# Sampling of the first image taken in turn with the offsets of the other three

## The chip, the cores and the metric

The kernel runs on one core of one Trainium2 chip. The metric is the device time of one execution in microseconds (us), lower is better. Before the change, three runs took 10536.02 to 10541.7 us, with a median of 10539.41 us. A core has five engines that run beside each other, each with its own queue of instructions in a fixed order: PE (matmul), DVE (vector), ACT (scalar functions), POOL (general) and SP (here it only starts transfers). Sixteen DMA engines move data between HBM and the core's SBUF.

## The reference

The input x holds four images of 64x64 positions with 256 channels. Layer 0 is a deformable convolution, layer 1 an attention and a feed-forward block with a choice of tokens. Only layer 0 is touched here. Cut to what matters:

```
def layer0(x):                                   # per image
    v = group_norm(x)                            # 32 groups of 8 channels
    xp = v @ in_w + in_b                         # projection that is sampled
    x1 = silu(batch_norm(depthwise_conv3x3(v)))
    offset = x1 @ off_w + off_b                  # 8 groups x 9 points x (x, y)
    mask = softmax(x1 @ mask_w + mask_b)         # over the 9 points
    out = sum over points of mask * bilinear(pad(xp), point + offset)
    return x + (out @ out_w + out_b)
```

An offset smaller than one position in size reaches only a 5x5 window around a position. The kernel therefore makes, for each position and group, 25 window weights out of mask and offset, and a sample is a weighted sum of 25 shifted copies of xp. The few positions with a larger offset are computed once more, exactly, by gathers.

## The kernel before, in words

The program is written as dataflow, and a scheduler decides at build time in which order each engine gets its instructions. It takes ready instructions by their place in the program, by a model of durations. What is wrapped in `keep` stays in the program's order on its engine. `Pinned` is a stand-in for `nc.vector` that wraps every DVE operation in `keep`.

**Offsets** (`offsets_and_weights`, L263) runs first, for all four images, with `slab` 8: an image is 32 tiles of 128 positions, worked on in four slabs of 8. Its parts:

- `front(n)` (L322): loads x in eight pieces (`xt`, L333, on SP's queue, three buffers), transposes them on PE, takes statistics on DVE (L341) and copies to `xn` on ACT; then group statistics, and the scaling of the whole of `xn` on ACT (L366). The front of the next image is advanced by one or two pieces after each slab.
- `convolution(s)` (L412): channel half 1 on PE by nine matmuls with diagonal matrices `diag` (L420), channel half 0 on DVE by nine multiply-adds (L432, L434), then silu on ACT.
- `taps(s)` (L437): offset and mask matmuls into `po` (L444), the sum `raw` on DVE (L448), the softmax's maximum and subtraction on DVE, its exponential on ACT (L458).
- `window(s)` (L461): the rest of the softmax (L463 to L465), the hat functions on ACT (L473 to L477), three rounds of `my`, `mxy` and sums into `w5` on DVE (L483 to L488), transposes on PE (L497) and the store of the weights `wt_d` (L501).
- `projection(i)` (L380): matmuls of a quarter of an image (L387), bias on ACT into `xp`, stores of `xp_d` (L398), transposes (L405), copies into `tb` on ACT (L406), and the store of the gather table `tab_d` (L407).

All stores are issued on SP. Per slab the program has convolution(s+1), taps(s), window(s), projections and the next front. [...] four for `a_t` (transposes), four for `a_m` (matmul results). `a_ld` (xt, tb, wT) has three buffers.

**Zero fill** (L1387 to L1397) follows: 24 stores on SP put zeros on the borders of `xp_d` and `tab_d`.

**Sampling of image 0** (`sample_image`, L668) runs alone after that, with depth 6. It is a generator with some 440 steps. `list_tokens` makes the list of positions with large offsets. Then for each of four chunks of 1024 positions and each channel half: the shifted source `xs` is loaded (L683, two buffers), and for each of 25 window places the weights `wb` are loaded with a broadcast (L688, twelve buffers) and multiplied with the source (L697, kept) and added to `ac` (L705, kept). Between them `exact_rows` gathers table rows with POOL's indirect DMAs (L626) and reduces them on DVE (L637, L640). At a chunk's end `ac` is multiplied with the output weights (L721), x and bias are added (L725, L728) and `t_d` is stored (L729).

**Attention and the rest** start with `t_d` of image 0. The sampling of image n+1 is taken in turn with attention of image n; there `sample_image` has depth 1, so `wb` has two buffers and `xs` and `ac` one.

The main program's part:

```
    with scope(
        ("a_one", 1, 0), ("a_xn", 2, 0), ("a_ld", 3, 0), ("a_wk", 2, 0), ("a_w1p", 1, 0), ("a_sm", 2, 0),
        ("a_t", 4, 1), ("a_m", 4, 1),
    ):
        offsets_and_weights(range(NB), SLAB, 2)
    ...
    with scope(("smp", 2, 0), ("two", 2, 0), ("sb", 2, 0), ("dn", 1, 0), ("ps_m", 2, 1)):
        for _ in sample_image(0, 6):
            pass
```

Of the kernel before, what the change touches and what calls it, by code (L numbers as in the profile page):

```python
# [16 lines left out]
P = 128  # L17
# [28 lines left out]
def layers_kernel(ctx: ExitStack, tc: tile.TileContext, a, out: bass.AP):  # L46
# [216 lines left out]
    def offsets_and_weights(images, slab, rows_bufs):  # L263

        ca = S.a_one
# [52 lines left out]
        diag = ca.tile([P, K2, P], F32, name="diag")  # L318
        for tap in range(K2):
            nc.vector.tensor_scalar(diag[:, tap], ident, dwk[:, 1, tap : tap + 1], None, ALU.mult)  # L320

        def front(n):  # L322
# [8 lines left out]
            for s in range(8):  # L331
                xt = S.a_ld.tile([P, 4, C], F32, tag="xt", name="xt")
                nc.sync.dma_start(  # L333
                    out=xt, in_=x_d[n, s * 512 : (s + 1) * 512].rearrange("(t p) c -> p t c", p=P)
                )
                for k in range(CC):
                    pt = S.a_t.tile([P, 4, P], F32, tag="pt", name="pt")
                    for t in range(4):
                        nc.tensor.transpose(pt[:, t, :], xt[:, t, k * P : (k + 1) * P], ident)
                    ptf = pt.rearrange("p t q -> p (t q)")  # L340
                    nc.vector.bn_stats(st[:, k, s, :], ptf)  # L341
                    nc.scalar.copy(
                        xn[:, k, 1 + 8 * s : 9 + 8 * s, 1 : 1 + W],
                        ptf.rearrange("p (r w) -> p r w", w=W),
                    )
                yield
            mv = S.a_sm.tile([P, CC, 2], F32, tag="mv", name="mv")
            for k in range(CC):
                nc.vector.bn_aggr(mv[:, k, :], st[:, k].rearrange("p s f -> p (s f)"))
# [5 lines left out]
            nc.vector.tensor_copy(gm, pg)  # L355
            gv = S.a_sm.tile([P, CC], F32, tag="gv", name="gv")
            nc.vector.tensor_sub(gv, mv[:, :, 0], gm)
            nc.vector.tensor_mul(gv, gv, gv)
            nc.vector.tensor_add(gv, gv, mv[:, :, 1])
# [3 lines left out]
            nc.vector.scalar_tensor_tensor(gm, gm, -1.0, gr, ALU.mult, ALU.mult)  # L363
# [7 lines left out]
        for _ in front(images[0]):  # L371
            pass
        for at, n in enumerate(images):
            xn = xns.pop(n)
            after = front(images[at + 1]) if at + 1 < len(images) else iter(())
# [4 lines left out]
            def projection(s):  # L380
# [16 lines left out]
                for f in range(CC):  # L397
                    nc.sync.dma_start(out=xp_d[n][f][:, q0 : q0 + 16 * MP], in_=xp[:, f, : 16 * MP])  # L398
                for o in range(0, 16 * MP, P):
# [7 lines left out]
                    nc.sync.dma_start(out=tabw[q0 + o : q0 + o + m], in_=tb[:m].rearrange("p f g c e -> p (f g c e)"))  # L407
# [4 lines left out]
            def convolution(s):  # L412
                x1 = S.a_wk.tile([P, CC, slab * P], F32, tag="x1", name="x1")
                x1s[s] = x1
                r0 = 2 * slab * s
                for o in range(0, slab * P, 512):
                    pc = S.a_m.tile([P, 8, W], F32, tag="pm", name="pc")
                    for tap in range(K2):
                        r = r0 + o // W + tap // 3
                        nc.tensor.matmul(  # L420
                            pc, diag[:, tap], xn[:, 1, r : r + 8, tap % 3 : tap % 3 + W],
                            start=(tap == 0), stop=(tap == K2 - 1),
                        )
                    nc.scalar.activation(
                        x1[:, 1, o : o + 512], pc.rearrange("p r w -> p (r w)"), AF.Silu,
                        bias=bnsh[:, 1:2], scale=bns[:, 1:2],
                    )
                acc = x1[:, 0].rearrange("p (r w) -> p r w", w=W)
                for tap in range(K2):
                    src = xn[:, 0, r0 + tap // 3 : r0 + tap // 3 + 2 * slab, tap % 3 : tap % 3 + W]  # L430
                    if tap == 0:
                        nc.vector.tensor_scalar(acc, src, dwk[:, 0, 0:1], None, ALU.mult)  # L432
                    else:
                        nc.vector.scalar_tensor_tensor(acc, src, dwk[:, 0, tap : tap + 1], acc, ALU.mult, ALU.add)  # L434
                nc.scalar.activation(x1[:, 0], x1[:, 0], AF.Silu, bias=bnsh[:, 0:1], scale=bns[:, 0:1])

            def taps(s):  # L437
                x1 = x1s.pop(s)
                raw = S.a_wk.tile([P, slab, 3 * GP], F32, tag="raw", name="raw")
                for t in range(0, slab, 2):  # L440
# [7 lines left out]
                    nc.vector.tensor_tensor(  # L448
# [7 lines left out]
                nc.vector.tensor_reduce(red, m3, AX.X, ALU.max)  # L456
                nc.vector.tensor_tensor(m3, m3, rbc, ALU.subtract)
# [3 lines left out]
            def window(s):  # L461
                raw, m3, red, rbc = raws.pop(s)
                nc.vector.tensor_reduce(red, m3, AX.X, ALU.add)  # L463
                nc.vector.reciprocal(red, red)
                nc.vector.tensor_tensor(m3, m3, rbc, ALU.mult)  # L465
# [10 lines left out]
                nc.vector.tensor_reduce(omax[:, n, s * slab : (s + 1) * slab], hat[:, 1], AX.X, ALU.max)  # L476
# [4 lines left out]
                for ey in range(3):  # L481
                    my = S.a_w1p.tile([P, slab, GP], F32, tag="my", name="my", bufs=2)
                    nc.vector.tensor_mul(my, raw[:, :, 2 * GP :], hat[:, ey, :, GP:])  # L483
                    for ex in range(3):
                        mxy = S.a_w1p.tile([P, slab, GP], F32, tag="mxy", name="mxy", bufs=2)
                        nc.vector.tensor_mul(mxy, my, hat[:, ex, :, :GP])
                        blk = w5[:, :, ex : ex + 3, ey : ey + 3]
                        nc.vector.tensor_tensor(  # L488
                            blk, blk, mxy.rearrange("p t (g i j) -> p (t g) i j", i=3, j=3), ALU.add
                        )  # L490

                w5t = w5.rearrange("p (t f g) i j -> p t f (g i j)", t=slab, f=CC)
                for t in range(0, slab, 4):
                    for f in range(CC):
# [6 lines left out]
                        nc.sync.dma_start(out=wt_d[n][f, :, o : o + 512], in_=wT[: GH * ND])  # L501
# [3 lines left out]
            for s in range(ns):  # L505
                if s + 1 < ns:
                    convolution(s + 1)
                taps(s)
                window(s)
                for i in range(s * (H // 16) // ns, (s + 1) * (H // 16) // ns):  # L510
                    projection(i)
                for _ in range(8 // ns):
                    next(after, None)
            for _ in after:
                pass

# [151 lines left out]
    def sample_image(n, depth=1):  # L668
# [9 lines left out]
        for c in range(L // CH):  # L678
            ac = S.dn.tile([P, CC, CH], F32, tag="ac", name="ac", bufs=min(depth, 2))
            for f in range(CC):  # L680
                xs = S.dn.tile([P, CH // W + 4, MP], F32, tag="xs2", name="xs2", bufs=min(depth, 2))
# [4 lines left out]
                for d in range(ND):  # L686
                    wb = S.dn.tile([P, CH], F32, tag="wb", name="wb", bufs=2 * depth)
# [6 lines left out]
                    else:  # L694
                        prt = S.dn.tile([P, CH], F32, tag="prd", name="prd", bufs=min(depth, 2))
# [685 lines left out]
    with scope(  # L1381
        ("a_one", 1, 0), ("a_xn", 2, 0), ("a_ld", 3, 0), ("a_wk", 2, 0), ("a_w1p", 1, 0), ("a_sm", 2, 0),
        ("a_t", 4, 1), ("a_m", 4, 1),
    ):
        offsets_and_weights(range(NB), SLAB, 2)

    with scope(("one", 1, 0)):  # L1387
        zm = S.one.tile([P, 2 * G * 2 * CG], F32, name="zm")
        nc.gpsimd.memset(zm, 0.0)
        for n in range(NB):  # L1390
            tabw = tab_d[n].rearrange("(q g) c -> q (g c)", g=G)
            for q0 in (0, (H + 2) * MP):
                for f in range(CC):
                    nc.sync.dma_start(out=xp_d[n][f][:, q0 : q0 + 2 * MP], in_=zm[:, : 2 * MP])
                nc.sync.dma_start(
# [3 lines left out]
    with scope(("smp", 2, 0), ("two", 2, 0), ("sb", 2, 0), ("dn", 1, 0), ("ps_m", 2, 1)):  # L1399
        for _ in sample_image(0, 6):  # L1400
# [77 lines left out]
```

## Time and profile before

| | us |
|---|---|
| Median of three runs | 10539.41 |
| The profiled execution | 10563.61 |
| Its span, first to last instruction | 10561.9 |
| Constants and first front, until the first convolution | 0 to 59 |
| Offsets of four images | 59 to 814 |
| Zero fill and list of positions | 814 to 872 |
| Sampling of image 0 | 872 to 1482 |
| Attention's preparation of image 0, then all the rest | from 1482 |

The profile records one execution. Over the whole span the engines are busy like this (busy us, share of the span, instructions):

```profile
PE 9008.4 (85%) x38460; PEld 4375.8 (41%) x38460; DVE 8547.2 (81%) x13406; ACT 7377.6 (70%) x8389; POOL 5265.2 (50%) x3059
```

Most of that is attention, so these shares say little of the first 1482 us. There one reads by stage. In a group's line, what stands after the second bar is how long the engine stood idle just before these instructions, and after the arrow who ended that idle time. PE's clock is granted[...]: 1.00 is full speed.

### The profile page before, as it was taken

To read this page: it belongs to the slowest core of one execution; us is meant where nothing else is said; L and a number is where in the kernel's file an instruction comes from. 1 tells how busy PE (TensorE), PEld (TensorE's weight loads), DVE (VectorE), ACT (ScalarE), POOL (GpSimd) and SP (SyncE) were. 2 spreads that over 40 slices of the span, in tenths; PEclk is the share of its full clock that TensorE was granted. 3 is DMA by queue.
4 is the path that set the end of the run, shared out by engine and by line. 5 is a ranking of instruction groups with operands and counts; after the bars stand their busy time and mean duration, and the time that the engine had idled before them with its cause. 6 is when DMAs were issued, how large, how long until landed. Compare 5 with 4: busy or idle time off the path is not lost. (4 is left out here: it accounts for less than half of the span.)

```text
span 10561.9 us, 115936 instructions
## 1 busy us (share of the span) xinstructions
PE 9008.4 (85%) x38460; PEld 4375.8 (41%) x38460; DVE 8547.2 (81%) x13406; ACT 7377.6 (70%) x8389; POOL 5265.2 (50%) x3059
## 2 busy tenths in 40 slices
PE   7882029999999678999999589999999699999995
PEld 4551014444444343444444344444444344444443
DVE  7776879898989778989899679899898357777772
ACT  4450018888888528888888438888888379999991
POOL 0004307676555326767655327676555155555552
PEclk8985569999999889999999789999999799999997
DMA  3336752222222252212111352222111300000002
GB/s 119 107 138 180 206 167 70 61 67 64 70 64 73 98 167 60 52 55 58 51 55 50 116 152 53 53 54 54 52 59 41 101 13 9 10 8 7 7 5 75
DMA packets 381330, 766.00 MB, mean 73 GB/s; under 512 B 49105, under 2 KB 212593, under 8 KB 380689
## 3 DMA queue, kind: packets, MB, share of 16 engines
q1 hardware_dynamic: 324432, 678.78, 20.3%
q0 software_dynamic: 30144, 45.87, 2.9%
q10 hardware_dynamic: 26112, 33.56, 0.9%
q8 instruction: 309, 5.06, 0.2%
q14 instruction: 333, 2.72, 0.1%
HBM read 580.88 MB, written 177.14 MB: 72 GB/s over the span
## 5 line engine op out<-in xcount | busy, mean ns | idle before, releaser
L909 DVE TENSOR_TENSOR r<-nn,r 128x512 f32<-128x512 f32 x6144 | 3943.0, 683 | 861.5 <-PE nn L904 805.9
L904 PE MATMUL nn<-qn,kf 32*128 32x512 f32 (+1 forms) x12288 | 4518.8, 640 | 132.7 <-DVE r L909 95.8
L994 POOL TENSOR_TENSOR r<-r 128x1024 f32<-128x1024 f32 x1024 | 2708.8, 2645 | 2645.4 <-DVE r L909 2625.3
L988 ACT ACTIVATE r<-d 128x1024 f32<-128x1024 f32 x3072 | 3117.2, 1015 | 1085.4 <-DVE r L998 699.9
L894 PE MATMUL d<-qf,kf 32*128 32x512 f32 (+1 forms) x12288 | 3338.1, 632 | 76.5 <-DMA qf<-qf 43.1
L990 ACT ACTIVATE r<-r 128x1024 f32<-128x1024 f32 x3072 | 3124.1, 1051 | 32.6
L904 PEld LDWEIGHTS nn<-qn,kf 32*128 32x128 f32 (+1 forms) x12288 | 1399.4, 185 | 1902.1 <-DVE r L909 1450.5
L932 PE MATMUL pv<-v,et 128*128 128x257 f32 x8192 | 2105.3, 400 | 15.0 <-DVE acv L956 15.0
L932 PEld LDWEIGHTS pv<-v,et 128*128 128x128 f32 x8192 | 1507.6, 194 | 975.5 <-issue 768.6
L894 PEld LDWEIGHTS d<-qf,kf 32*128 32x128 f32 (+1 forms) x12288 | 1018.0, 186 | 1340.3 <-issue 736.1
L996 POOL TENSOR_TENSOR r<-r 128x512 f32<-128x512 f32 x1024 | 1335.8, 1304 | 92.7 <-DVE r L909 17.1
L705 DVE TENSOR_TENSOR ac<-ac,prd 128x1024 f32<-128x1024 f32 x768 | 991.8, 1291 | 8.8
L697 DVE TENSOR_TENSOR prd<-xs,wb 128x1024 f32<-128x1024 f32 x768 | 977.7, 1273 | 15.2 <-DMA wb<-wt 12.0
L626 POOL DMA_INDIRECT ga<-tab,tii x576 | 718.3, 1247 | 207.3 <-issue 117.7
L916 ACT ACTIVATE et<-et,nshift 128x512 f32<-128x512 f32 x1024 | 723.8, 707 | 28.2 <-DVE et L1001 28.2
L998 DVE TENSOR_TENSOR r<-r 128x512 f32<-128x512 f32 x1024 | 723.6, 707 | 4.1 <-POOL r L994 3.7
L1001 DVE TENSOR_TENSOR et<-r 128x512 f32<-128x512 f32 x1024 | 698.1, 682 | 0.4
L115 ACT ACT_TABLE_LOAD x9 | 11.5, 1283 | 799.3 <-DVE mv L259 703.0
L721 PE MATMUL pmo<-outwp,ac 128*128 128x256 f32 x512 | 135.7, 416 | 469.1 <-DVE ac L705 431.2
L480 POOL MEMSET w<- 128x1600 f32 x16 | 22.9, 1432 | 675.0 <-PE ptw L497 352.3
L721 PEld LDWEIGHTS pmo<-outwp,ac 128*128 128x128 f32 x512 | 100.8, 205 | 521.4 <-DVE ac L705 304.5
L420 PE MATMUL pc<-xn,diag 128*128 128x512 f32 x576 | 262.2, 609 | 33.4 <-ACT xn L366 33.4
(344 smaller groups left out, 5282.7 us busy)
## 6 DMA issues: line engine op xcount, KB each, us to landing
wb<-wt SPq DMA_DIRECT2D x800, 512.0 KB
tab<-tb SPq DMA_DIRECT2D x128, 256.0 KB
v<-t SPq DMA_DIRECT2D x64, 512.0 KB
xs<-xp SPq DMA_DIRECT2D x32, 680.0 KB
xp<-xp SPq DMA_DIRECT2D x32, 544.0 KB
xt<-in_x_dram SPq DMA_DIRECT2D x32, 512.0 KB
xr<-in_x_dram SPq DMA_DIRECT2D x64, 256.0 KB
t<-xr SPq DMA_DIRECT2D x64, 256.0 KB
```

Of the source, the lines that this page charges most:

```text
L697: keep(nc.vector.tensor_tensor(pr.rearrange("p (r w) -> p r w", w=W), src, wb.rearrange("p (r w) -> p r w", w=W), ALU.mult,))
L705: keep(nc.vector.tensor_add(ac[:, f, :], ac[:, f, :], pr))
L894: keep(nc.tensor.matmul(d[:, j, :], kf[g, blk, rows(kt)], qs[q][0][g, blk, :], start=True, stop=True))
L904: keep(nc.tensor.matmul(nn, kf[g, blk, rows(kt)], qs[q][1][g, blk, :], start=True, stop=True))
L909: keep(nc.vector.tensor_tensor(r[:, j, :], ns[j], r[:, j, :], ALU.mult))
L916: keep(nc.scalar.activation(ets[b], ets[b], AF.Exp, bias=nshift))
L932: keep(nc.tensor.matmul(pv, ets[b0 + i][:, rows(j)], v[:, k0 + i, :], start=(i == 0), stop=(i == PVB - 1)))
L988: keep(nc.scalar.activation(rs[b, p], ds.pop((b, p)), AF.Ln))
L990: keep(nc.scalar.activation(rs[b, p], rs[b, p], AF.Exp, scale=-1.0))
L994: keep(nc.gpsimd.tensor_tensor(rs[b, 1], rs[b, 1], rs[b, 2], ALU.add))
L996: keep(nc.gpsimd.tensor_tensor(rs[b, 1][:, 0], rs[b, 1][:, 0], rs[b, 3][:, 0], ALU.add))
L998: keep(nc.vector.tensor_add(rs[b, 1][:, 1], rs[b, 1][:, 1], rs[b, 3][:, 1]))
```

## The change

The sampling of image 0 no longer waits for the offsets of all images. `offsets_and_weights` becomes a generator. It runs image 0 to its end (`next(others)`), and then the offsets of images 1 to 3 and the sampling of image 0 are advanced in turn: after each of five places in a slab, three or four steps of sampling.

With that go these edits:

- slabs of four tiles in place of eight;
- for images 1 to 3 both channel halves of the convolution run on PE (`diag` holds both); image 0 keeps half 0 on DVE;
- taps(s) stands ahead of convolution(s+1);
- for images 1 to 3 the DVE operations are pinned to the written order (`vec`);
- x is loaded on POOL's queue; the stores of projection, table, window weights and the zero fill are issued on ACT's queue; sampling's loads and stores and the store of `raw` stay on SP;
- fewer buffers: `wb` 2 for 12, `xs` and `prd` 1 for 2, `a_ld` 2 for 3, `my` and `mxy` 1 for 2, `xp` 1 for 2; PSUM 3 + 3 + 2 banks, where offsets had 4 + 4;
- the zero fill stands before the offsets.

```diff
-        diag = ca.tile([P, K2, P], F32, name="diag")
-        for tap in range(K2):
-            nc.vector.tensor_scalar(diag[:, tap], ident, dwk[:, 1, tap : tap + 1], None, ALU.mult)
-
-        def front(n):
+        diag = ca.tile([P, CC, K2, P], F32, name="diag")
+        for k in (1, 0):
+            for tap in range(K2):
+                nc.vector.tensor_scalar(diag[:, k, tap], ident, dwk[:, k, tap : tap + 1], None, ALU.mult)
+
+        def front(n, vec):
...
-                nc.sync.dma_start(
+                nc.gpsimd.dma_start(
                     out=xt, in_=x_d[n, s * 512 : (s + 1) * 512].rearrange("(t p) c -> p t c", p=P)
                 )
...
-        for _ in front(images[0]):
+        for _ in front(images[0], nc.vector):
             pass
         for at, n in enumerate(images):
             xn = xns.pop(n)
-            after = front(images[at + 1]) if at + 1 < len(images) else iter(())
+            vec = pinned if at else nc.vector
+            after = front(images[at + 1], vec) if at + 1 < len(images) else iter(())
...
-                    nc.sync.dma_start(out=xp_d[n][f][:, q0 : q0 + 16 * MP], in_=xp[:, f, : 16 * MP])
+                    nc.scalar.dma_start(out=xp_d[n][f][:, q0 : q0 + 16 * MP], in_=xp[:, f, : 16 * MP])
...
-                    nc.sync.dma_start(out=tabw[q0 + o : q0 + o + m], in_=tb[:m].rearrange("p f g c e -> p (f g c e)"))
+                    nc.scalar.dma_start(out=tabw[q0 + o : q0 + o + m], in_=tb[:m].rearrange("p f g c e -> p (f g c e)"))
...
+                for k in range(CC):
+                    if k == 0 and not at:
...
+                                vec.scalar_tensor_tensor(
+                                    acc, src, dwk[:, 0, tap : tap + 1], acc, ALU.mult, ALU.add
+                                )
+                        nc.scalar.activation(x1[:, 0], x1[:, 0], AF.Silu, bias=bnsh[:, 0:1], scale=bns[:, 0:1])
+                        continue
+                    for o in range(0, slab * P, 512):
+                        pc = S.a_m.tile([P, 8, W], F32, tag="pm", name="pc")
+                        for tap in range(K2):
+                            r = r0 + o // W + tap // 3
+                            nc.tensor.matmul(
+                                pc, diag[:, k, tap], xn[:, k, r : r + 8, tap % 3 : tap % 3 + W],
+                                start=(tap == 0), stop=(tap == K2 - 1),
+                            )
...
                         blk = w5[:, :, ex : ex + 3, ey : ey + 3]
-                        nc.vector.tensor_tensor(
+                        vec.tensor_tensor(
                             blk, blk, mxy.rearrange("p t (g i j) -> p (t g) i j", i=3, j=3), ALU.add
                         )
+                    yield
...
-                        nc.sync.dma_start(out=wt_d[n][f, :, o : o + 512], in_=wT[: GH * ND])
+                        nc.scalar.dma_start(out=wt_d[n][f, :, o : o + 512], in_=wT[: GH * ND])
...
             for s in range(ns):
+                taps(s)
                 if s + 1 < ns:
                     convolution(s + 1)
-                taps(s)
-                window(s)
+                if at:
+                    yield
+                for _ in window(s):
+                    if at:
+                        yield
                 for i in range(s * (H // 16) // ns, (s + 1) * (H // 16) // ns):
                     projection(i)
                 for _ in range(8 // ns):
                     next(after, None)
+                if at:
+                    yield
             for _ in after:
                 pass
+            if not at:
+                yield
...
-    def sample_image(n, depth=1):
+    def sample_image(n, sums=1):
...
-            ac = S.dn.tile([P, CC, CH], F32, tag="ac", name="ac", bufs=min(depth, 2))
+            ac = S.dn.tile([P, CC, CH], F32, tag="ac", name="ac", bufs=sums)
...
-                xs = S.dn.tile([P, CH // W + 4, MP], F32, tag="xs2", name="xs2", bufs=min(depth, 2))
+                xs = S.dn.tile([P, CH // W + 4, MP], F32, tag="xs2", name="xs2")
...
-                    wb = S.dn.tile([P, CH], F32, tag="wb", name="wb", bufs=2 * depth)
+                    wb = S.dn.tile([P, CH], F32, tag="wb", name="wb", bufs=2)
...
-        offsets_and_weights(range(NB), SLAB, 2)
...
-    with scope(("smp", 2, 0), ("two", 2, 0), ("sb", 2, 0), ("dn", 1, 0), ("ps_m", 2, 1)):
-        for _ in sample_image(0, 6):
+    with scope(
+        ("a_one", 1, 0), ("a_xn", 2, 0), ("a_ld", 2, 0), ("a_wk", 2, 0), ("a_w1p", 1, 0), ("a_sm", 2, 0),
+        ("smp", 2, 0), ("two", 2, 0), ("sb", 2, 0), ("dn", 1, 0), ("a_t", 3, 1), ("a_m", 3, 1), ("ps_m", 2, 1),
+    ):
+        others = offsets_and_weights(range(NB), SLAB // 2, 1)
+        next(others)
+        first = sample_image(0, 2)
+        for at, _ in enumerate(others):
+            for _ in range((4, 4, 3, 3, 4)[at % 5]):
+                next(first, None)
+        for _ in first:
             pass
```

## The prediction

> **What bounds the kernel now.** I read the 40 slices of the page first, then the table of busy times by stage, then the groups and waits of the two stages that the change touches. The end of the page's chain (attention, feed-forward) is untouched, so what counts is how early the work at 1482 us can start.
>
> ```profile
> PE   7882029999999678999999589999999699999995
> DVE  7776879898989778989899679899898357777772
> ACT  4450018888888528888888438888888379999991
> ```
>
> A digit is the busy share of 264 us. Slices 1 to 3 hold the offsets of four images: PE is high, DVE near 7. Slices 4 and 5 hold the first image's sampling: PE and ACT fall to 2 and 0, DVE carries on alone. Two stages with different limits stand one after the other.
>
> ```profile
> core 0: us, PE busy (x) PEld busy (x) DVE busy (x) ACT busy (x) POOL busy (x), PEclk, DMA share, GB/s
> 59.00:252.00 193.00, 158.43 (x613) 95.66 (x614) 138.85 (x185) 96.27 (x164) 6.79 (x12) 0.90 0.37 127
> 252.00:440.00 188.00, 160.84 (x612) 97.68 (x612) 134.58 (x181) 90.34 (x161) 6.80 (x12) 0.89 0.38 130
> 814.00:872.00 58.00, 33.16 (x136) 31.55 (x136) 23.81 (x103) 0.00 (x0) 0.00 (x0) 0.50 0.53 181
> 872.00:1482.00 610.00, 44.40 (x134) 32.80 (x134) 511.31 (x464) 0.00 (x0) 205.37 (x162) 0.53 0.66 191
> ```
>
> An image of offsets takes 188 to 193 us with PE busy for 83% of it. The zero fill and token list take 58 us with no engine full. Sampling takes 610 us, 511 of them DVE. The whole up to 1482 is 59 + 755 + 58 + 610.
>
> ```profile
> L705 DVE TENSOR_TENSOR ac<-ac,prd 128x1024 f32<-128x1024 f32 x192 | 238.0, 1240 | 6.5
> L697 DVE TENSOR_TENSOR prd<-xs,wb 128x1024 f32<-128x1024 f32 x192 | 234.9, 1223 | 0.0
> L728 DVE TENSOR_TENSOR xr<-pmo,xr 128x512 f32<-128x512 f32 x16 | 11.1, 692 | 43.7 <-POOL xr L725 29.8 <-PE pmo L721 13.3 <-PE pso L649 0.5
> L637 DVE TENSOR_TENSOR ga<-ga,wg 128x1152 f32<-128x1152 f32 x8 | 10.9, 1358 | 41.9 <-DMA ga<-tab,tii 41.9
> ```
>
> These are the groups of sampling alone. Multiplies and adds are 473 us and never wait for the weights wb (0.0 idle), with twelve wb buffers. What DVE waits for is the gather (41.9) and the closing sum (43.7).
>
> ```profile
> DVE raw L448 <- PE po L444: 23.1, 5, 15.4
> DVE st L341 <- PE pt L339: 17.7, 6, 12.3
> DVE red L463 <- ACT raw L458: 5.4, 2, 3.2
> ```
>
> These are DVE's waits in the first image of offsets. They sum to 54 us of idle with the smaller ones; about 24 of it is the gap between images (the last pt, group statistics, the scaling of xn at L366, first convolution).
>
> **What the skill says.** "Perfetto Trace Analysis", Optimization Strategy, says that where the most contended engine changes over time, interleaving the regimes may help; the two middle rows above agree (PE 158 of 193, then DVE 511 of 610). "DMA: Bandwidth & Descriptors", Issuing engines are not separate DMA queues, says that loads begun on several engines share the same 16 engines and save only issue time. So I give the three queues no bandwidth; the trace has SP issues of 0.3 to 0.6 us. "TensorE: Matmul & The Clock Gate", What's actually happening, says an idle array falls to half its clock; the trace agrees, 0.53 in sampling against 0.90 in the offsets. More PE work beside sampling can run at the high clock.
>
> **The change, part by part.** All sums are against the profiled execution, 10563.6 us (span 10561.9); the median shown is 24 us lower.
>
> *Start.* Zero fill moves to the start, on ACT's queue. There it cost 28 us of SP issue (813.8 to 844); ACT's first copy of xn is at 33.5 us, so it is hidden. If that cover fails, up to 10 us. x loads go to POOL, with two buffers for three. The last stretch of the first image's loads is 33 to 47 us; a slower round trip costs 0 to 15 us; I take 8. Nine more diagonal matrices (L320, 0.28 us each) fall into DVE's idle time. First convolution at 67 instead of 59.
>
> *First image.* Same engines as now, in slabs of four tiles. Two back-to-back 128x576 operations take 1.42 us with 0.75 for the second, a pitch of 0.67, against 1.14 for 128x1024 in the sampling rows of the timeline: 1.05 ns an element and 0.066 us fixed. Four more slabs of some 36 DVE instructions add 10 us of DVE, where 54 are idle; finer steps shorten the run-in. I take 190 us (range 180 to 205): 257.
>
> *Run-in of the second image.* 18 convolution matmuls at 0.59, two silus of 0.78 with a table load of 1.28, four po matmuls of 0.35: 15 us. DVE's fixed order puts the first multiply behind the first raw sum, so sampling starts at 272, not 872.
>
> *The joint stage*: sampling of image 0 with images 1 to 3, in DVE's written order. DVE work: sampling 511 plus one token list 12 (half of the 23.8 above) is 523. An image has 134.6 less its own convolution on DVE, 44 (42 to 41 in L434, 3 in L432), or 91; three are 272, less one front of 11 that now runs in the first image: 261. Twelve more slabs times 27 instructions times 0.066 us: 21. Sum 805. Then what this order leaves idle: between images, nothing of sampling stands between the group statistics and the next raw sum, so DVE waits for the scaling of xn and the first convolution and taps, 27 us (the 8.35 of PE for xn, 15 as above, and statistics), twice: 54. xs has one buffer for two: seven changes at about 4 us: 28 (0 to 60). Other waits for PE and ACT, 30 us an image now, part covered by four sampling steps of 1.2 us behind the softmax's subtraction: 20 an image, 60 (20 to 150). Sum 947, say 950.
>
> *Does PE fit?* An image has 158 plus its second half of convolutions, 144 matmuls, 65.5 us (a quarter of L420's 262): 223. Three, with pmo 42 and the list 8, are 720 of 950, 76%, less than 83% today. Taps ahead of the next convolution give DVE its raw sum while PE convolves.
>
> *Does the data fit?* 200 loads of wb in 950 us are one in 4.75. Two buffers allow a round trip of two pitches less a multiply. Image 1's sampling already runs with two, beside attention's preparation:
>
> ```profile
> 1559.14 1.22 DVE L697 TENSOR_TENSOR prd<-xs,wb 128x1024 f32<-128x1024 f32 x1
> 1560.36 1.23 DVE L259 TENSOR_REDUCE least<-pk 128x1 f32<-128x1024 f32 x1
> 1561.50 1.22 DVE L705 TENSOR_TENSOR ac<-ac,prd 128x1024 f32<-128x1024 f32 x1
> 1563.21 0.75 DVE L259 TENSOR_SCALAR mm<-pq,bqk 128x512 f32<-128x512 f32 x1 [0.50 <-PE pf L833]
> 1563.88 1.22 DVE L697 TENSOR_TENSOR prd<-xs,wb 128x1024 f32<-128x1024 f32 x1
> ```
>
> One multiply in 4.7 us and no wait for a load, with 208 GB/s in that stretch. So the round trip is at most 2 x 4.7 - 1.2 = 8.2 us there, and my pitch just fits.
>
> *ACT and POOL.* ACT takes over an image's 36 table, 16 weight and 8 projection stores: 60 issues of 0.35 us, 21 us on top of 90, and twice the switches of its tables (1.28 us each). About 130 of 317 us an image; it hides, unless one store blocks what stands behind it. Each store waits for ACT's own copy, and two tb buffers for three let ACT wait for landings (24 us in all now). Behind ACT stand the exponentials and hats that DVE needs; this is in the 60 above, and in the second rival. POOL has 181 us of gathers, the memsets and 16 x loads: hidden; the gather's 41.9 us of DVE wait go, since a group's multiplies now span twice the time, and are not in my 805.
>
> *Sum.* 272 + 950, and 14 from the last sum to the last store (1467.5 to 1482): 1236. That is 246 less than 1482. Nothing after it changes: 10563.6 - 246 = 10318, less 24 for the median: 10295 us. Own range 10230 to 10370.
>
> **Rivals.**
> Nearly full packing: waits within an image vanish and the xs changes are covered. The stage is 870 and the time 10215. For: 24 slabs with much to fill; against: DVE reached only 88% in its easiest hundred microseconds of sampling.
> A second engine's order decides: ACT blocked at table stores, or PE held at its three PSUM banks (a_m) while po waits for DVE. An extra 5 us in each of 24 slabs plus a few us a projection is 130: stage 1080, time 10425. For: 24 us of tb waits today with three buffers; against: PE 76%, ACT near 40%.
> Slower: wb's two buffers set the pace. The joint stage becomes 200 times half of (round trip plus 1.2 us). It equals the old end when the stage is 1196 us, 5.98 a load, a round trip of 10.7 us. At 12 us the stage is 1320 and the time about 10665. For: table, weight and image transfers now compete, SP's queue also holds raw and t stores that wait for DVE (69.6 us behind L729 today), and a queued store delays every wb behind it; against: the rows above.
> The change doesn't interleave: waits put most of sampling behind the offsets still, and PE pays 197 us more of convolution: about 10560.
>
> **How the numbers follow.** Forecast 0.55, full packing 0.16, second engine 0.17, slower by wb 0.09, no interleaving 0.03. The range takes in most of the first three: 10200 to 10440. A difference under 0.2%, some 21 us, can't be told from none. Faster 0.88, same 0.02, slower 0.10.
>
> **What would show it.** The stage table: first multiply near 272; DVE over 80% busy from there to the start of attention's preparation near 1240; PE near 76% with a clock over 0.85 there; no slices with PE at 0 to 2. L697's idle before it, put down to wb, stays under 30 us; if it is hundreds, the wb rival holds. L448's and L463's idle in hundreds means PE or ACT. An image gap over 40 us, or an xs change over 9, breaks those terms. A start after 320 means that the first image or the x loads on POOL cost more than I gave.

## The result, and the profile after

| | before | after |
|---|---|---|
| Median of 11 runs each, us | 10536.02 | 10558.12 |
| Ratio, 95% interval | | 1.0027 [1.0019, 1.0035] |
| Span of the profiled execution, us | 10561.9 | 10554.0 |
| First convolution starts, us | 59.3 | 104.5 |
| First raw sum of image 1, us | | 343.0 |
| Last sum with bias and x (`xr`) of image 0's sampling starts, us | 1481.2 | 1498.1 |
| Attention's preparation starts, us | 1498.4 | 1514.7 |

The changed kernel is 22 us slower by the medians (28 by the ratio); the forecast was 246 us less. What comes after the start of attention's preparation takes 9064 us in the profiled execution before and 9039 in the one after, so the two spans can't be compared directly: the times of the two starts can, and they give 16 us of the 22.

The forty slices of the page after, for three engines:

```profile
PE   6767659999999788999999689999999699999995
DVE  6667779898989778989899679899898357777772
ACT  4323227888888637888888438888888379999991
```

The slices with PE at 0 to 2 are gone, so the two stages do run beside each other. But DVE has only 6 and 7 in the first six slices, where the forecast wanted over 80%. Nothing is full there. The table of busy times by stage, in the same columns as before (the first row goes from the first to the second image's first convolution, the second from the first raw sum of image 1 to the last sum of sampling; PEclk, the third number from the end, is PE's granted clock):

```profile
104.50:323.00 218.50, 177.38 (x681) 110.24 (x681) 169.61 (x407) 112.44 (x196) 18.60 (x30) 0.88 0.40 131
343.00:1498.00 1155.00, 755.62 (x2288) 403.17 (x2286) 847.91 (x1173) 330.73 (x559) 189.02 (x186) 0.81 0.52 162
```

In the second row DVE, the third busy time, is busy for 848 of 1155 us and PE for 756. DVE stands still for 307 us. The view of DVE's waits between 310 and 1498 us tells for whom: engine, what it is about to do, what it waits for, us in total, times, the longest:

```profile
DVE st L259 <- PE pt L343: 147.1, 16, 17.9
DVE raw L259 <- PE po L454: 73.1, 6, 23.9
DVE prd L716 <- DMA wb<-wt: 27.5, 23, 2.4
DVE xr L747 <- POOL xr L744: 23.2, 7, 9.0
```

(All pinned operations are recorded under the helper's line, L259.) The second line holds three waits of 24 us at the images' starts, the third is the wait for weights, small as forecast. The first is new in its size: 147 us in which DVE waits for the transposes of x in the next image's front. In the offsets before the change the same wait was this, over all four images:

```profile
DVE st L341 <- PE pt L339: 53.4, 20, 13.5
```

Eight of the waits after the change are 15 to 18 us long, one in every second slab of images 1 and 2. The timeline of one, with start, duration, engine, line, what is made out of what, and in brackets the idle time before it and who ended it:

```profile
603.63 0.37 ACT L411 COPY tb<-ptc 128x256 f32<-128x256 f32 x1 [4.44 <-DMA tab<-tb]
604.06 0.69 PE L410 MATMUL ptc<-ident,xp 128*128 128x128 f32 x2 [4.13 <-ACT tb L411]
...
610.72 0.69 PE L410 MATMUL ptc<-ident,xp 128*128 128x128 f32 x2 [0.86 <-ACT tb L411]
...
614.71 1.11 PE L343 MATMUL pt<-ident,xt 128*128 128x128 f32 x4 [0.46 <-ACT tb L411]
615.86 0.70 DVE L259 BATCH_NORM_STATS2 st<-pt 128x6 f32<-128x512 f32 x1 [17.41 <-PE pt L343]
```

PE works through the table transposes of a projection (`ptc`), and waits between them for ACT to empty PSUM, which waits for a store of the table. The front's transpose (`pt`), 1.1 us of work, stands behind them in PE's queue. DVE's next operation in the written order is the statistics of that transpose, so for 17.4 us no sampling goes ahead either; the next multiply, at 619.0 us, then starts without a wait for its weights. The projection comes in every second slab, and the last image has no next front: that is why there are eight.

The start, from the same timeline:

```profile
26.64 0.95 POOL L1403 MEMSET zm<- 128x1024 f32 x1 [0.55 <-DVE slotr L223]
...
54.61 2.06 ACTq L1409 DMA_DIRECT2D tab<-zm  x1
...
62.19 0.20 POOL L308 MEMSET gavg<- 128x128 f32 x1 [34.59 <-DMA tab<-zm]
...
65.90 0.56 PE L276 MATMUL pb<-inb,perm 128*128 128x2 f32 x2 [39.73 <-DMA wom<-in_L_conv_mask_w_dram]
```

The zero tile's memory is handed on to the constants of the offsets. These are loaded or made only when the last zero store has landed, at 62 us. POOL waits 34.6 us for that, and PE 39.7. ACT's queue issues the stores until 56.7 us.

### The profile page after: what moved, and what is told of

The parts are those of the page before. It is cut to its first block, busy times and chain, and to the rows that moved or that the text cites. A ratio compares the mean times of both kernels' runs of the same rounds, so it can differ in the third digit from the quotient of the medians.

```text
span 10554.0 us, 117389 instructions
## 1 busy us (share of the span) xinstructions
PE 9291.3 (88%) x38892; PEld 4491.2 (43%) x38892; DVE 8500.4 (81%) x13775; ACT 7457.2 (71%) x8519; POOL 5257.5 (50%) x3106
## 5 line engine op out<-in xcount | busy, mean ns | idle before, releaser
L645 POOL DMA_INDIRECT ga<-tab,tii x576 | 686.0, 1191 | 313.8 <-DVE so L659 169.5
L438 PE MATMUL pc<-xn,diag 128*128 128x512 f32 x1008 | 466.5, 613 | 47.4 <-ACT xn L370 22.1
L490 POOL MEMSET w<- 128x800 f32 x32 | 24.6, 769 | 602.4 <-PE ptw L508 589.0
L438 PEld LDWEIGHTS pc<-xn,diag 128*128 128x128 f32 x1008 | 193.8, 197 | 273.3 <-issue 210.9
L1319 POOL DMA_INDIRECT sort<-v,rif x128 | 124.1, 969 | 304.1 <-DVE rif L259 189.0
L1380 ACT ACTIVATE big<-ph,b 128x512 f32<-128x512 f32 x128 | 87.4, 685 | 261.8 <-PE ph L1379 261.5
```

## The experiments

Ratios are against the kernel before, whose time each set of runs measured again on its chip; the changed kernel stands at 1.0027 [1.0019, 1.0035]. A difference of 0.001 is 10.5 us. The intervals reach 8 to 18 us to each side, so a difference of two kernels is uncertain by 12 to 25 us. The last column is a second reading, from one profiled execution each.

| kernel | ratio, 95% interval | us against the changed kernel | attention's preparation starts, us |
|---|---|---|---|
| e1_front_first | 0.9951 [0.9934, 0.9967] | -80 | 1440.1 |
| e1_tb4 | 1.0025 [1.0018, 1.0033] | -2 | 1516.2 |
| e1_wb3 | 1.0019 [1.0010, 1.0028] | -8 | 1504.2 |
| e1_zero_later | 1.0007 [0.9998, 1.0015] | -21 | 1498.2 |
| e2_sp | 1.0002 [0.9994, 1.0011] | -26 | 1495.6 |
| e2_pairs | 0.9913 [0.9897, 0.9930] | -120 | 1401.7 |
| e2_gap | 0.9875 [0.9858, 0.9891] | -160 | 1366.8 |
| e2_all | 0.9811 [0.9794, 0.9827] | -228 | 1291.1 |
| e3_early | 0.9806 [0.9790, 0.9822] | -233 | 1277.8 |
| e3_early_sp | 0.9788 [0.9772, 0.9804] | -252 | 1264.5 |
| e3_half_dve | 0.9934 [0.9918, 0.9951] | -98 | 1432.9 |
| e3_conv_first | 0.9871 [0.9855, 0.9888] | -164 | 1337.6 |

The third column is the difference of the ratios times 10536 us. The changed kernel's attention starts at 1514.7.

### Who holds the front's transposes?

My theory after the trace: the order in PE's queue. Rivals: the landing of table stores with two `tb` buffers, and the two buffers of weights. The first kernel writes the next front ahead of the projection:

```diff
+                for _ in range(8 // ns):
+                    next(after, None)
                 for i in range(s * (H // 16) // ns, (s + 1) * (H // 16) // ns):
                     projection(i)
-                for _ in range(8 // ns):
-                    next(after, None)
```

> The next image's front is put ahead of the projection in each slab; no work is added or removed. Theory 'order on PE' (DVE's pinned statistics L345 stand behind 18 table transposes whose pace the table stores set, eight times 16 to 18 us): the waits of DVE for pt fall from 147 us to under 30, and the time from 10558 to about 10450. Theory 'two wb buffers set the pace': no change beyond 10 us, waits for wb take the place. Theory 'PE is simply full': the wait moves to po (raw), DVE's idle stays near 330 us and the time within 30 us of 10558.

80 us faster than the changed kernel, where the first theory asked for some 108. DVE's waits for `pt` and for the other releasers of the same statistics sum to 3.6 us in this stage, from 147. What is left of the stage's larger waits (DVE's waits of this kernel from 318 to 1425 us):

```profile
DVE raw L259 <- PE po L454: 52.0, 4, 25.6
DVE prd L716 <- DMA wb<-wt: 30.9, 23, 3.7
DVE raw L259 <- remote: 28.2, 1, 28.2
...
DVE gm L259 <- PE pg L357: 19.4, 2, 9.8
```

("remote" is a releaser that the profile doesn't name; it stands at the first raw sum of image 1.) A projection has no DVE operation, so DVE's written order is the same as before this edit: the place of the transposes behind the projection is the cause of these waits. The edit moves ACT's copies out of PSUM with them, and PE's queue and ACT's aren't told apart by it. ACT's waits for table stores are still 83.8 us in the stage (86.8 in the changed kernel's), so their late landing alone doesn't hold DVE. Of the 147 us a part comes back in other places (gm, the group statistics behind the same queue, has 19.4 where it had 1.5). The second kernel gives the table's rows four buffers; `inw` and `womr` move into working buffers to make room, here and in each kernel below that takes more memory (e1_wb3, e2_pairs, e2_all and those built on it):

```diff
-                    tb = S.a_ld.tile([P, CC, GH, 2, CG], F32, tag="tb", name="tb")
+                    tb = S.a_ld.tile([P, CC, GH, 2, CG], F32, tag="tb", name="tb", bufs=4)
```

> Four tb buffers for two, order unchanged (two constants that are read once share other tiles' room to make space). 'Order on PE' with the store's landing as the pace: ACT's wait for the table stores falls from 71 us to under 15, each of the eight long waits for pt from about 16.5 to 8 us, the time to about 10490. If the pace of the chain is PE and ACT handing over, and not the landing: less than 25 us gained.

No difference. ACT's waits for table stores fall from 71 to 16 us (310 to 1400 us), the long waits for the front's transposes fall only to 11 to 13 us (one of 18.7 remains), and the stage from the first multiply to the last sum gains 25 us, which a longer first image takes back (first multiply at 332.9 in place of 310.8; ahead of it DVE now waits 26.6 us for the front of image 1, where it waited 2.6). So the stores' landing makes the queue slower, but the place in the queue decides. The third gives weights three buffers:

```diff
-                    wb = S.dn.tile([P, CH], F32, tag="wb", name="wb", bufs=2)
+                    wb = S.dn.tile([P, CH], F32, tag="wb", name="wb", bufs=3 if n == 0 else 2)
```

> Three wb buffers for two in the first image's sampling. Theory 'two wb buffers set the pace': a gain of 100 us or more. 'Order on PE': only the 24 us that DVE shows as waits for wb can go, most of it taken up elsewhere; the time between 10530 and 10560.

8 us, which the two intervals don't tell from none. DVE's waits for weights are gone from the trace, and the waits for `pt` stand at 148.1 as before. The weights' two buffers don't hold the stage.

### The start

The zero fill is written behind the first image, out of a buffer of sampling, on SP's queue:

```diff
+        next(others)
+        zm = S.dn.tile([P, 2 * G * 2 * CG], F32, tag="ga", name="zm")
...
-                nc.scalar.dma_start(
+                nc.sync.dma_start(
```

> The zero fill comes after the first image, from a tile that shares the gather's room, on SP's queue. If the late start (first convolution at 104 us where before had 59) is due to the fill's memory being handed on and its 24 stores ahead of everything: first convolution near 60 to 67, time about 10515. If it is due to loading x on POOL with two buffers: no earlier than 95, and under 12 us gained.

21 us, half of what was expected. The first convolution starts at 78.0 in place of 104.5, not near 60 to 67; attention's preparation starts 16.5 us earlier. In time the stores have not moved back: SP issues them from 13 to 45 us, since the scheduler takes what is ready. What has changed is that the constants no longer take over their memory, and that ACT's queue is free of them:

```profile
27.08 0.20 POOL L308 MEMSET gavg<- 128x128 f32 x1 [0.55 <-DVE slotr L223]
...
44.47 0.36 SPq L1414 DMA_DIRECT2D tab<-zm  x1
```

POOL makes `gavg` at 27.1 us, which in the changed kernel waited until 62.2. Memory and queue were changed together; that it is the memory is read from the traces, no run parts the two. The start is 19 us later than before the change even so. PE's timeline of this kernel shows waits of 8.9, 5.4 and 2.1 us for the x loads issued on POOL.

### Who issues the stores?

The stores of projection, table and window weights are issued on SP again:

```diff
-                    nc.scalar.dma_start(out=xp_d[n][f][:, q0 : q0 + 16 * MP], in_=xp[:, f, : 16 * MP])
+                    nc.sync.dma_start(out=xp_d[n][f][:, q0 : q0 + 16 * MP], in_=xp[:, f, : 16 * MP])
...
-                    nc.scalar.dma_start(out=tabw[q0 + o : q0 + o + m], in_=tb[:m].rearrange("p f g c e -> p (f g c e)"))
+                    nc.sync.dma_start(out=tabw[q0 + o : q0 + o + m], in_=tb[:m].rearrange("p f g c e -> p (f g c e)"))
...
-                        nc.scalar.dma_start(out=wt_d[n][f, :, o : o + 512], in_=wT[: GH * ND])
+                        nc.sync.dma_start(out=wt_d[n][f, :, o : o + 512], in_=wT[: GH * ND])
```

> The changed kernel with the stores of projection, table and window weights issued on SP's queue again, as before the change. Theory that PE's order holds the stage and ACT's issuing does not: within 20 us of the changed kernel (ratio 1.001 to 1.005), the long waits for the front's transposes stay at 15 to 18 us. Rival, that ACT is blocked by the stores in its own queue: at least 50 us faster (ratio under 0.998), the long waits fall. Third, that SP's stores then stand before the loads of weights: slower by 50 us or more, with L707's loads late and DVE waiting for wb by 100 us or more.

26 us less, a little outside the band of the first theory and half of what the rival asked. The waits for `pt` stay near where they were (DVE, 298 to 1481 us):

```profile
DVE st L259 <- PE pt L343: 134.7, 16, 19.1
```

DVE's wait for wb grows only from 27.5 to 32.5 us. So issuing these stores on ACT costs some 26 us, 12 of them ahead of the first multiply (298.7 against 310.8), and SP had room for them.

### Small operations that need one another

On top of e1_front_first, the three weights of a round get a buffer each, and a sum no longer stands right behind its weight:

```diff
+                        mxy = S.a_w1p.tile([P, slab, GP], F32, tag="mxy", name="mxy", bufs=3)
...
+                    weight(0)
+                    weight(1)
+                    add(0)
+                    weight(2)
+                    add(1)
+                    add(2)
```

> The kernel with the next front ahead of the projection, and in each round of the window the three weights mxy get a buffer each and are written in the order weight, weight, sum, weight, sum, sum, so that no DVE operation needs the result of the one just before it. Theory that pairs of dependent small operations cost 0.49 us each instead of 0.34: seven operations of a round take 2.5 us instead of 3.3, three rounds in 24 slabs give back 45 us; DVE's busy time of the joint stage falls from 858 to about 815 us, and the time is about 0.4% below the kernel with the front ahead (ratio near 0.991). Rival, that an operation of 128x288 costs this much whatever stands before it: no change, ratio 0.995.

40 us below e1_front_first, as the theory said (attention starts 38 us earlier: from the first multiply to the last sum DVE's busy time falls by 25 us, where 43 were expected, and its idle time by 6, and 7 come ahead of the first multiply). The changed kernel's timeline, where each weight stands right ahead of its sum:

```profile
351.28 0.46 DVE L259 TENSOR_TENSOR mxy<-my,hat 128x288 f32<-128x288 f32 x1
351.77 0.46 DVE L259 TENSOR_TENSOR w<-w,mxy 128x288 f32<-128x288 f32 x1
352.26 0.46 DVE L259 TENSOR_TENSOR mxy<-my,hat 128x288 f32<-128x288 f32 x1
```

and that of e2_pairs:

```profile
353.06 0.82 DVE L259 TENSOR_TENSOR mxy<-my,hat 128x288 f32<-128x288 f32 x2
353.80 0.45 DVE L259 TENSOR_TENSOR w<-w,mxy 128x288 f32<-128x288 f32 x1
354.17 0.45 DVE L259 TENSOR_TENSOR mxy<-my,hat 128x288 f32<-128x288 f32 x1
354.54 0.94 DVE L259 TENSOR_TENSOR w<-w,mxy 128x288 f32<-128x288 f32 x2
```

Where an operation doesn't need the one just before it, it starts 0.37 us after that one's start; where it does, or has to wait for the single `mxy` to be read, 0.49. A round of seven takes 2.83 us (352.57 to the next multiply at 355.40) instead of 3.33 (449.28 to 452.61 in the changed kernel), and 72 such rounds would give 36 us.

### The images' starts

On top of e1_front_first, twenty sampling steps between the group statistics and the first raw sum of an image, and four, three, three, three, three steps at the five places of a slab:

```diff
             for s in range(ns):
+                if at and s == 0:
+                    yield 20
                 taps(s)
...
-            for _ in range((4, 4, 3, 3, 4)[at % 5]):
+            for _ in range(more or (4, 3, 3, 3, 3)[turn % 5]):
```

> The kernel with the next front ahead of the projection, and 20 sampling steps put between an image's group statistics and its first raw sum. Theory that the three waits at image starts (25 to 28 us each, 80 together) are DVE's written order and nothing else: they fall below 10 us each, the time is about 50 us under the kernel with the front ahead (ratio near 0.990), and the first sampling multiply comes some 15 us earlier. Rival, that DVE merely does the same work earlier and waits for PE in the following slab: ratio 0.995 as there, with new waits of the same sum elsewhere.

80 us below e1_front_first, more than the 50 expected. DVE's waits for `po` fall from 80 us (52.0 and 28.2) to 9.9:

```profile
DVE raw L259 <- PE po L454: 9.9, 3, 9.1
```

The first multiply did not come 15 us earlier, as expected, but at 317.0 (317.6 there); what comes earlier is everything behind it, since only a handful of sampling operations stood ahead of the first raw sum. A new wait of 24.7 us appears at the end of the stage, for the last table stores of image 3.

### All together, and what holds the stage then

e2_all has zero fill, front, pairs and gap as above, and the first image's x loads on SP.

> All repairs together: zero fill after the first image, the first image's x loads on SP's queue, the next front ahead of the projection, sums not right behind their weights, 20 sampling steps between an image's statistics and its first raw sum. If the pieces add: 20 to 30 us for the zero fill, 10 for the x loads, 80 for the front's place, 40 for the pairs, 50 for the gap, together 200 to 210 us below the changed kernel, ratio near 0.983; first convolution at 60 to 66 us, first multiply near 260, attention's preparation near 1310. If they cover one another (DVE gains time only to wait for PE, whose work of 760 us does not shrink): 100 to 130 below, ratio near 0.991.

228 us below the changed kernel. The single steps (21, 80, 40, 80) sum to 221; by the starts of attention's preparation it is 224 for the whole and 203 for the four. The x loads, which were not run alone, bring the first convolution from 78.0 to 68.8. So within these readings the gains add. The stretch from the end of the first image to the last sum, in the columns of the tables above:

```profile
260.00:1277.00 1017.00, 747.41 (x2354) 405.61 (x2353) 834.30 (x1219) 339.22 (x570) 208.26 (x207) 0.85 0.62 188
```

DVE is now busy for 82%. What has come up in place of the old waits is the one at the end, 24.8 us here, and gm with 23.3. The next kernel has each projection one slab earlier:

```diff
-                for i in range(s * (H // 16) // ns, (s + 1) * (H // 16) // ns):
+                for i in range(-(-s * (H // 16) // ns), -(-(s + 1) * (H // 16) // ns)):
```

> The kernel with all repairs, whose trace ends the joint stage with 24.8 us in which DVE waits for the last table stores of image 3; here each projection stands one slab earlier (slabs 0, 2, 4, 6 in place of 1, 3, 5, 7). If this tail is only the late place of the last projection: 20 us less, ratio near 0.979. If the projections then press on PE beside the convolution at an image's start: no gain, ratio 0.981, with a longer wait there.

The tail is gone from the trace and attention starts 13 us earlier; in the times the two ratios can't be told apart (0.9806 and 0.9811, intervals of 0.0016 to each side). A new wait of 18 us for the output matmuls of sampling stands in PE's queue at 1027.8 us. With the stores on SP as well:

> The same, and the stores of projection, table and window weights on SP's queue. In the unrepaired kernel this gave back some 12 us of the first image and 12 us of the joint stage. If ACT's issuing costs that here too: ratio near 0.977. If SP's queue delays the loads of weights now that the stage is 170 us shorter: ratio 0.981 or more, DVE's wait for wb over 60 us (23 in the kernel with all repairs).

The fastest kernel: 10307.3 us beside 10534.2 for the kernel before, 2.1% less. It can't be told from e3_early by the intervals. DVE's wait for weights is 37.6 us, under the 60 that would have told against SP.

Two parts of the change were undone within e2_all. Channel half 0 of the convolution on DVE again:

```diff
-                    if k == 0 and not at:
+                    if k == 0:
```

> The kernel with all repairs, with channel half 0 of the convolution of images 1 to 3 on DVE again, as before the change (pinned, right behind the offset sums). PE loses 432 matmuls, some 200 us, DVE gains 3 images of some 44 us, 132 us. If DVE holds the joint stage: 100 to 130 us slower than with all repairs, ratio 0.990 to 0.994. If PE and its order hold it: the same or faster, ratio 0.981 or less.

0.0123 more, 130 us. The stage:

```profile
265.00:1408.00 1143.00, 618.15 (x1894) 365.73 (x1895) 987.44 (x1434) 346.99 (x563) 218.62 (x207) 0.73 0.54 166
```

DVE has 153 us more work, PE 129 less (200 were expected; the granted clock is 0.73 for 0.85), and the stage is 126 longer, while DVE's idle time falls from 183 to 156 us: it is DVE's work that holds it, and moving this half to PE is worth some 130 us once the order is right. And the next convolution written ahead of the offset matmuls:

```diff
+                if s + 1 < ns:
+                    convolution(s + 1)
                 taps(s)
-                if s + 1 < ns:
-                    convolution(s + 1)
```

> The kernel with all repairs, with the convolution of the next slab written ahead of the offset matmuls of this one again, as before the change. The 18 convolution matmuls of a slab are 10.6 us of PE. If their place ahead of the offset matmuls delays the first raw sum beyond the few sampling steps that DVE has before it: 3 to 5 us in each of 24 slabs, 70 to 120 us slower than with all repairs, ratio 0.988 to 0.993, with DVE's waits for po in the tens. If PE runs far enough ahead of DVE: the same, ratio 0.981.

0.0060 more, 63 us (46 by the start of attention), under the band of the first theory. DVE's waits for `po` go from 5.6 to 53.4 us, but in three places at the images' starts (26.1, 10.5 and 14.3 us), not in every slab as I had expected: within an image PE runs far enough ahead.

## Why the prediction was wrong

The forecast was 10295 and the time is 10558. The stage was to end at 1236 us, and its last sum starts at 1498, 262 later. The overlap came about as it said; what it had too small were the waits inside it, and the start. By its own steps:

- **Start**, "so it is hidden. If that cover fails, up to 10 us", and 8 us for the x loads: 67 forecast, 104.5 measured. The prediction asked when ACT first had work of its own, not whose memory the zero tile takes; and ACT issued the stores until 56.7 us, well past the 33.5 that was to hide them. The zero fill as it was written costs 26.5 us of start (e1_zero_later). Of the 19 us that stay, 9 go with the x loads on POOL, by the step from e1_zero_later to e2_all, where other edits are in too, so the 8 may have been right; the last 10, still there in e2_all, no run explains. Plus 37.5 us.
- **First image and run-in**, 190 and 15: from the first convolution to the first raw sum of image 1 are 238.5 us, not 205. The run-in is 20 us for 15. The prediction put 18 convolution matmuls ahead of the first raw sum, which is one channel half of a slab; by its own count of 144 for a half in eight slabs there are 36, and PE's timeline has them in 17.8 us (below). The first image is 218.5 us for 190. DVE's work in it is 169.6 us, 31 more than in the same stretch before; some 12 of that are the list of positions and some 5 sampling itself, which the prediction had in the joint stage. Its marker for this step, the first multiply near 272 or after 320, was poor: that multiply was to come behind the first raw sum, but three multiplies and one sum came ahead of it, from 298.5 us on, before DVE stood for 23.9 us until 343.0. Plus 33.5 us. No run took this term apart; e2_sp shows 12 us of it as ACT's issuing.
- **DVE's work**, 805: 848. The 848 do not even hold the 17 us of list and sampling named above, so like for like it is some 60 us more. The term of "twelve more slabs times 27 instructions times 0.066 us" was taken from neighbours that don't need one another. In the written order most operations of the window do, and then the fixed part is 0.19 us (0.49 less 288 x 1.05 ns). Plus 43 us. The Trainium skill's "Perfetto Trace Analysis", Optimizing Scalar/DVE Operations, has about 60 ns a DVE operation on SBUF, and a profiled latency of about twice that "since the write-acknowledgement half overlaps with the next instruction". The trace agrees on the first, 0.066 us where there is no need. The record of one operation (0.45 us) has 0.15 beside its 288 elements, two and a half times the page's 60 ns, and with a need the next one starts only after the whole of it. e2_pairs gave back 40 us by the order and two more buffers.
- **Idle time**, 54 between images, 28 for xs, 60 for "other waits for PE and ACT", 14 at the end, 156 in all: 307. This is the step that failed: the 60 was to hold every wait within the images, and the waits for `pt` alone were 147. PE's 76% seemed to leave room; the prediction did not ask which pinned DVE operation reads what PE makes behind a row of slow work in its queue. The sign was in the lines that it shows: in the first image DVE waits 17.7 us for `pt`, 12.3 of them at once. It put that wait down to the gap between images. But in the timeline before, it stands at 236.8 us behind the same table transposes, and with a front piece written behind a projection in every second slab, and DVE pinned, it came eight times. Plus 151 us. With the front ahead of the projection 80 came back. Whether DVE's operations left free to the scheduler would have avoided the waits was not tried.

The convolution matmuls of the run-in, in one line of PE's timeline:

```profile
322.95 17.76 PE L438 MATMUL pc<-xn,diag 128*128 128x512 f32 x36 [4.59 <-ACT xn L370]
```

The four make 265, against 262 found; the 3 between are the prediction's rounding of 947 to 950.

Right were: the overlap itself; the gaps between images, 24 us each with the one at image 1's start counted in the run-in (27 forecast); weights with two buffers (27.5 us of waits, and no clear gain from a third buffer); xs (2.9 us of waits, less than the 28); PE's load, 755.6 busy for 720, though at a granted clock of 0.81 where over 0.85 was to show. The rival of the second engine came nearest in kind: it priced 130 us for waits on PE and ACT, but put them in ACT's stores and PSUM banks and in each slab. And its end, 10425, lacked the start. The rival "The change doesn't interleave" had 10560 and met the time by luck: sampling ran beside the offsets from 298.5 us on. What the smaller PSUM shares and the other single buffers cost was not tried.

Two readings of the prediction were off without bearing on the sum: the zero stores before took 30 us of SP's issue, not 28, single ones up to 2.5 us; and DVE was busy for 89% from 1300 to 1400 us and for 49.3 of the 50 us after that, so "only 88%" was too low as a case against full packing.

"Perfetto Trace Analysis", Optimization Strategy, which I took for the interleaving, goes on to say that one should find the gaps on the engine in question and what blocks it there. That held here: the gaps were found so, one after the other. With them repaired, attention starts at 1264.5 us (e3_early_sp), 234 earlier than before, and the time is 223 us less by the ratio. That this is near the forecast 246 doesn't bear the forecast out: the repairs also took away waits that it had counted, such as the gaps between images, and the late start is in part still there.

## What to carry to other kernels

When two streams of work are woven into one engine in a written order, each operation in that order becomes a gate for both: list for every pinned operation the last instruction that it waits for, and what stands ahead of that in its producer's queue. Write short producers (a transpose of the next block) ahead of long ones that others hold up (a table that is stored as it is made), and put other work where a stream has a chain through several engines. Before a step is moved to the start, see whose memory it takes and who gets that memory next.

## What the runs showed of the hardware

- A DVE operation of 128x288 f32 started 0.37 us after the start of its neighbour where it needed nothing of it, 0.49 where it read its result or overwrote the buffer that it read (changed kernel and e2_pairs).
- The 24 zero stores, 3.34 MB from one tile, took from 27.6 to 62.2 us to issue and land at 96 GB/s, with single issues on ACT's queue of up to 2.4 us; the same queue's table stores later took 0.33 us to issue.
- PE's granted clock was 0.55 in a stretch of the changed kernel where PE was busy for 24 of 80 us (640 to 720 us). Over the joint stage it was 0.73 with PE busy for 54% (e3_half_dve), against 0.85 with 73% in e2_all.
